# A graph network on one Trainium2 core: the adjacency products as two 64-row tiles of TensorE

## The chip, the cores and the metric

The kernel runs on one core of a Trainium2 chip. The metric is the time of the whole kernel on the device, in microseconds, median of three runs. A separate execution was recorded by the hardware profiler. Five engines work side by side: TensorE (PE in the profile, with its weight loads in a row of their own, PEld), VectorE (DVE), ScalarE (ACT), GpSimd (POOL) and SyncE (SP), which issues most of the transfers.

## The reference

The input x holds 128 graphs of 64 nodes with 256 features in 32-bit floats. One 64 x 64 adjacency matrix is shared by all graphs. Four layers follow one another, each adding to x what it makes of relu(layernorm(x)):

```python
# layer 0
h = relu(einsum('ts,bsh->bth', adj, x @ Wg0 + bg0))
h = relu(einsum('ts,bsh->bth', adj, h @ Wg1 + bg1))
for p in 1..4: an LSTM over windows of p nodes replaces the last node of each window
# layer 1
agg = einsum('nm,bmd->bnd', A_hat, features)
h = relu(batchnorm(agg @ W1.T + b1)); out = batchnorm(h @ W2.T + b2)
# layer 2
h = einsum('bjf,kfo->kbjo', x, W)
out = diag(adj) h[0] + triu(adj, 1) h[1] + tril(adj, -1) h[2] + bias
# layer 3: causal attention within a graph, with adj added to the scores
```

A_hat is the adjacency matrix with the identity added and rows and columns scaled by their degrees. The change concerns the products with adj in layer 0 (two of them) and with A_hat in layer 1.

## The kernel before

The 8192 rows (128 graphs x 64 nodes) are cut into 16 blocks of 512 rows. A block lies in on-chip memory as four groups q of 128 rows, which are two graphs each, with 256 features; features are handled as two chunks c of 128. All products are in 32-bit floats.

`aggregate` (line 180) multiplies a block by a node matrix. The matrix is held block-diagonally, 128 x 128 with the 64 x 64 matrix twice on the diagonal and zeros elsewhere (`block_diag`, line 90: `adjT_bd` for layer 0; `ahT`, line 126, for layer 1), so that one product serves two graphs. For each chunk c and each group q, line 186 takes the 128 rows of the input as the stationary operand (128 rows x 128 features) and the matrix as the moving one (128 columns). The four products of one c fill one PSUM bank, and one VectorE copy (line 187) brings the bank to `g`. The result is transposed, features on the partitions, as the next product with a weight matrix needs it. Every write starts and ends its own accumulation.

Who calls it: `graph_part` (line 229) works through layer 0's graph network for one block in five steps. The first loads x and normalises it (`layernorm_relu`, line 162: statistics on VectorE in lines 169 to 173, a power on GpSimd in line 172, four activations on ScalarE in line 176). The second makes `g0` with `aggregate`. The third multiplies by Wg0 (line 241), with an addition on VectorE (243) and a relu on ScalarE (245). The fourth makes `g1` with `aggregate`. The fifth multiplies by Wg1 (line 252), with line 255 on VectorE and 258 on ScalarE. `first_product` (line 390) does the first half of layer 1 in four steps: a load and a GpSimd copy (395); a transposition with identity (`to_token_major`, 196, with an addition on VectorE in 197), a store of the sum and the normalisation; `ag` with `aggregate`; the product with W1 (407), a ScalarE activation out of PSUM (410) and statistics on VectorE (411).

The order is written out by hand: `pipelined` (line 214) keeps one generator for each block, starts a new one in each round, and lets every live one take one step per round, the newest first. So a round of layer 0 holds, on PE's queue, `g0` of one block, line 241 of the block before, `g1` of the one before that and line 252 of the fourth, and what one step makes is used in the next round. PSUM has eight banks, handed out in turn (`bank`, line 65); a round of layer 0 and a round of layer 1 take eight each.

Between the two lies the LSTM (lines 288 to 360, the product in line 329), which takes over half of the time, and after layer 1 come layers 2 and 3 (`rest`, line 447). None of these calls `aggregate`.

Of the kernel before, what the change touches and what calls it, by code (L numbers as in the profile page):

```python
# [14 lines left out]
P = 128  # L15
# [5 lines left out]
def kernel(ctx: ExitStack, tc: tile.TileContext, a: dict, out: bass.AP):  # L21
# [4 lines left out]
    nc = tc.nc  # L26

    x = a["x"]
    B, T, D = x.shape
    NT = B * T  # L30
    KC = D // P
    SUP = 512
    NS = NT // SUP
    Q = SUP // P
# [30 lines left out]
    def bank():  # L65
        return psum.tile([P, 512], F32, tag="ps", name="ps")
# [113 lines left out]
    def aggregate(pool, h, mT, tag):  # L180

        g = pool.tile([P, KC, SUP], F32, tag=tag, name=tag)
        for c in range(KC):
            p_ = bank()
            for q in range(Q):
                nc.tensor.matmul(p_[:, ts(q, P)], h[:, q, ts(c, P)], mT, start=True, stop=True)
            nc.vector.tensor_copy(g[:, c, :], p_)
        return g

    def to_token_major(src, add, dst):  # L190
# [36 lines left out]
    with tc.tile_pool(name="pa", bufs=2) as pa, tc.tile_pool(name="pax", bufs=3) as pax:  # L227

        def graph_part(s):
            xt = pax.tile([P, Q, D], F32, tag="xt", name="xt")  # L230
            nc.sync.dma_start(xt, x_r[s])
            h = layernorm_relu(pa, xt)
            yield
            g0 = aggregate(pa, h, adjT_bd, "g0")
            yield
            h1 = pa.tile([P, Q, D], F32, tag="h1", name="h1")
# [8 lines left out]
            nc.scalar.activation(h1, h1, AF.Relu)  # L245
            yield
            g1 = aggregate(pa, h1, adjT_bd, "g1")
            yield
            for o in range(KC):
# [17 lines left out]
    with tc.tile_pool(name="wt", bufs=1) as wt:  # L267
# [5 lines left out]
        for k in range(3):  # L273
            p_ = bank().rearrange("p (d c) -> p d c", d=KC)
# [4 lines left out]
        for left, right, to in ((0, wT[:, KC : 2 * KC, :], wqk), (2, wo, wvo)):  # L279
            p_ = bank().rearrange("p (c m) -> p c m", c=KC)  # L280
            for c in range(KC):
                for d in range(KC):
                    nc.tensor.matmul(p_[:, c, :], wT[:, left * KC + d, ts(c, P)], right[:, d, :],
                                     start=(d == 0), stop=(d == KC - 1))
# [95 lines left out]
    with tc.tile_pool(name="pz", bufs=1) as pz:  # L380
# [9 lines left out]
        def first_product(s, pb, pbx):  # L390
            xt = pbx.tile([P, Q, D], F32, tag="xt", name="xt")
            nc.sync.dma_start(xt, x_r[s])
            hs = pb.tile([P, KC, SUP], F32, tag="hs", name="hs")
            for c in range(KC):
                nc.gpsimd.tensor_copy(hs[:, c, :].rearrange("p (b t) -> p b t", t=T), graphs(s, c))  # L395
            x1 = pbx.tile([P, Q, D], F32, tag="x1", name="x1")
            yield
            to_token_major(lambda c, q: hs[:, c, ts(q, P)], xt, x1)
            nc.sync.dma_start(x1d[s], x1)
            h = layernorm_relu(pb, x1)  # L400
            yield
            ag = aggregate(pb, h, ahT, "ag")
            yield
            for o in range(HC):
                p_ = bank()
                for c in range(KC):
                    nc.tensor.matmul(p_, w1[:, c, ts(o, P)], ag[:, c, :],  # L407
                                     start=(c == 0), stop=(c == KC - 1))
                z = zslot(s, o)
                nc.scalar.activation(z, p_, AF.Identity, bias=bn1[:, 0, o : o + 1])  # L410
                nc.vector.bn_stats(st1[:, o, s, :], z)
            yield
# [169 lines left out]
```

## Time and profile before

| | |
|---|---|
| median of three runs | 2158.73 us (2157.87 to 2158.78) |
| the profiled execution's own time | 2156.58 us |
| its span in the trace | 2154.9 us |
| TensorE clock granted, mean | 0.991 of full speed |
| PE busy | 2098.7 us, 97% of the span |
| VectorE busy | 791.4 us, 37% |
| ScalarE busy | 739.0 us, 34% |
| line 186, layer 0, busy on PE | 33.8 us (first product) and 31.2 us (second), 256 records each |
| line 186, layer 1, busy on PE | 43.4 us, 256 records |
| line 187, the copies, busy on VectorE | 41.4 us in layer 0, 20.4 us in layer 1 |

How to read it: the profile counts a matmul as busy from its start to its modelled end, so records of a row overlap, and the distance from start to start tells the pace. A row of groups shows line, engine, operation, what is written from what, sizes, count, busy time, mean duration, and the idle time of the engine before them with what ended it. A row of the timeline shows start, length and count of neighbouring records merged, and idle time before them in brackets. Layer 0's graph network runs from about 17 to 188 us, the first half of layer 1 from about 1385 to 1560 us.

### The profile page before, as it was taken

The page shows a single profiled execution, that of the slowest core. Times are in us where ns is not written, and L with a number is a line of the kernel's source. Part 1 is how long each engine was busy: PE and PEld are TensorE (multiplying, and loading weights), DVE is VectorE, ACT ScalarE, POOL GpSimd, SP SyncE. Part 2 cuts the span into 40 slices and gives each one's busy share as a digit, 9 for nine tenths or more (in the row PEclk, how much of TensorE's full clock was granted, in tenths as well). Part 3 has the DMA queues.
Part 4 walks back from the last instruction along what each step waited for, and adds up shares of the span by engine and source line. Part 5 has one row for each costly group of instructions (what it writes and reads, how often), then busy time and mean ns, then how long its engine had stood idle before and what let it go on. Part 6 is the DMA issues. An engine that isn't in the chain of part 4 may idle for free. (4 is left out here: it accounts for less than half of the span.)

```text
span 2154.9 us, 18142 instructions
## 1 busy us (share of the span) xinstructions
PE 2098.7 (97%) x7232; PEld 1247.9 (58%) x7232; DVE 791.4 (37%) x1569; ACT 739.0 (34%) x1267; POOL 139.2 (6%) x126
## 2 busy tenths in 40 slices
PE   6998999999999999999999999899999799999998
PEld 6775444444445666666444444455534577777777
DVE  6773222122112121122111111377634555555553
ACT  3553445233233233233222322244480133333332
POOL 1000000000000000000000000122100121111110
PEclk9999999999999999999999999999999899999999
DMA  5100000000001000000000000133200101111101
GB/s 192 58 20 20 0 0 20 0 0 0 0 0 40 0 1 0 1 0 1 0 0 0 0 0 0 59 98 98 76 0 0 41 9 40 40 40 40 40 30 40
DMA packets 35973, 54.23 MB, mean 25 GB/s; under 512 B 2608, under 2 KB 29488, under 8 KB 35888
## 3 DMA queue, kind: packets, MB, share of 16 engines
q1 hardware_dynamic: 31856, 49.29, 7.0%
q10 hardware_dynamic: 4032, 3.78, 0.6%
q8 instruction: 57, 0.93, 0.2%
q14 instruction: 28, 0.23, 0.0%
HBM read 36.28 MB, written 16.78 MB: 25 GB/s over the span
## 5 line engine op out<-in xcount | busy, mean ns | idle before, releaser
L329 PE MATMUL ps<-hT,wih 128*128 128x512 f32 (+2 forms) x2016 | 808.9, 541 | 0.0
L329 PEld LDWEIGHTS ps<-hT,wih 128*128 128x128 f32 x2016 | 383.0, 190 | 378.5 <-issue 313.3
L329 PE MATMUL ps<-hn,whh 128*128 128x512 f32 (+2 forms) x1152 | 466.3, 527 | 0.0
L329 PEld LDWEIGHTS ps<-hn,whh 128*128 128x128 f32 x1152 | 218.9, 190 | 200.4 <-issue 153.1
L176 ACT ACTIVATE ln_h<-x,ln_rn 128x256 f32<-128x256 f32 x192 | 99.7, 590 | 367.3 <-DVE ln_rn L173 362.3
L341 DVE TENSOR_TENSOR gi<-gi,gg 128x1024 f32<-128x1024 f32 (+2 forms) x36 | 38.2, 1062 | 385.6 <-ACT gg L331 385.6
L331 ACT ACTIVATE gi<-ps,lbias 128x512 f32<-128x512 f32 (+2 forms) x144 | 91.9, 638 | 234.4 <-PE ps L329 234.4
L331 ACT ACTIVATE gg<-ps,lbias 128x512 f32<-128x512 f32 (+2 forms) x144 | 91.9, 638 | 232.0 <-PE ps L329 232.0
L478 PE MATMUL ps<-wl,ag 128*128 128x256 f32 x768 | 168.4, 379 | 0.0
L478 PEld LDWEIGHTS ps<-wl,ag 128*128 128x128 f32 x768 | 144.7, 190 | 19.0
L331 ACT ACTIVATE go<-ps,lbias 128x512 f32<-128x512 f32 (+2 forms) x144 | 91.2, 634 | 89.3 <-PE ps L329 86.9
L338 DVE TENSOR_TENSOR cell<-gi,gg 128x1024 f32<-128x1024 f32 (+2 forms) x36 | 41.1, 1143 | 201.2 <-ACT gg L331 201.2
L395 POOL COPY hs<-hT 128x512 f32<-128x512 f32 x32 | 33.7, 1083 | 1228.0 <-PE ps L329 1228.0
L407 PE MATMUL ps<-ag,w 128*128 128x512 f32 x256 | 112.3, 592 | 0.0
L331 ACT ACTIVATE gf<-ps,lbias 128x512 f32<-128x512 f32 (+2 forms) x72 | 44.8, 622 | 164.9 <-PE ps L329 164.9
L342 DVE TENSOR_TENSOR cell<-gf,cell 128x1024 f32<-128x1024 f32 (+2 forms) x36 | 38.2, 1062 | 171.4 <-ACT gf L331 171.4
L172 POOL TENSOR_TENSOR ln_rn<-ln_rn,mhalf 128x4 f32<-128x4 f32 x64 | 64.6, 1009 | 565.3 <-DVE ln_rn L171 565.3
L344 ACT ACTIVATE gg<-cell 128x1024 f32<-128x1024 f32 (+1 forms) x72 | 68.7, 954 | 82.2 <-DVE cell L343 82.2
L467 PE MATMUL ps<-adj,ln_h 128*128 128x384 f32 x256 | 88.2, 499 | 6.1 <-ACT ln_h L176 6.1
L351 DVE TENSOR_TENSOR hT<-go,gg 128x512 f32<-128x512 f32 (+2 forms) x72 | 47.1, 654 | 86.7 <-ACT go L331 62.4
L407 PEld LDWEIGHTS ps<-ag,w 128*128 128x128 f32 x256 | 47.5, 190 | 54.0 <-issue 50.7
L169 DVE BATCH_NORM_STATS2 ln_st<-x 128x6 f32<-128x256 f32 x192 | 76.9, 401 | 0.0
(127 smaller groups left out, 1965.4 us busy)
## 6 DMA issues: line engine op xcount, KB each, us to landing
xt<-in_x_dram SPq DMA_DIRECT2D x32, 512.0 KB, 4.5
x1d<-x SPq DMA_DIRECT2D x16, 512.0 KB, 3.0
x<-x1d SPq DMA_DIRECT2D x16, 512.0 KB, 4.5
out_dram<-x SPq DMA_DIRECT2D x16, 512.0 KB, 3.2
wih<-in_WihT_dram SPq DMA_DIRECT2D x4, 1024.0 KB, 6.3
whh<-in_WhhT_dram SPq DMA_DIRECT2D x3, 1024.0 KB, 7.5
wqkv<-in_Wqkv_dram ACTq DMA_DIRECT2D x1, 768.0 KB, 4.2
wl<-in_W_dram ACTq DMA_DIRECT2D x3, 256.0 KB, 3.2
```

The source lines that it names most:

```text
L169: nc.vector.bn_stats(st[:, q, :], src[:, q, :])
L172: nc.gpsimd.tensor_tensor(rn[:, 0, :], rn[:, 0, :], mhalf[:, :Q], ALU.pow)
L176: nc.scalar.activation(h[:, q, :], src[:, q, :], AF.Relu, bias=rn[:, 1, q : q + 1], scale=rn[:, 0, q : q + 1])
L329: nc.tensor.matmul(o_, w[:, c, ts(m, P)], r, start=(n == 0), stop=(n == len(ops) - 1))
L331: nc.scalar.activation(gt[:, hc, :N], p_[:, :N], fn, bias=lbias[:, l, m : m + 1])
L338: nc.vector.tensor_mul(c_, i_, g_)
L341: nc.vector.tensor_mul(i_, i_, g_)
L344: nc.scalar.activation(g_, c_, AF.Tanh)
L351: nc.vector.tensor_mul(cols(blk, c, j), gate["o"][:, c, :N].rearrange("p (w b) -> p w b", b=GB), gate["g"][:, c, :N].rearrange("p (w b) -> ...
L407: nc.tensor.matmul(p_, w1[:, c, ts(o, P)], ag[:, c, :], start=(c == 0), stop=(c == KC - 1))
L467: nc.tensor.matmul(p_, h[:, q, ts(c, P)], adj3.rearrange("p k n -> p (k n)"), start=True, stop=True)
L478: nc.tensor.matmul(p_[:, q, :], ag[:, c, k, ts(q2 + q, P)], wl2[k][:, c, :], start=(n == 0), stop=(n == 3 * KC - 1))
```

## The change

The two graphs of a group are multiplied apart. The stationary operand is the 64 rows of one graph (64 rows x 128 features), the moving one the 64 x 64 block of the matrix on the same rows (64 columns). Rows 0 to 63 and 64 to 127 of the array are two tiles, and each tile writes a bank of its own[...]. A bank now holds all chunks and groups of one graph of each pair, so the two copies come after all products and write runs of 64 elements. An aggregate has 16 products in the code where it had 8, and two copies as before. In the built program 384 products stand on rows 0 to 63 and 384 on rows 64 to 127, where 384 on 128 rows stood; the order of the other instructions on each engine is the same.

```diff
@@ -180,11 +180,17 @@
     def aggregate(pool, h, mT, tag):
 
         g = pool.tile([P, KC, SUP], F32, tag=tag, name=tag)
+        half = [bank().rearrange("p (c q n) -> p c q n", c=KC, q=Q) for _ in range(2)]
+
         for c in range(KC):
-            p_ = bank()
             for q in range(Q):
-                nc.tensor.matmul(p_[:, ts(q, P)], h[:, q, ts(c, P)], mT, start=True, stop=True)
-            nc.vector.tensor_copy(g[:, c, :], p_)
+                for b in range(2):
+                    r = slice(b * T, (b + 1) * T)
+                    nc.tensor.matmul(half[b][:, c, q], h[r, q, ts(c, P)], mT[r, r],
+                                     start=True, stop=True)
+        for b in range(2):
+            to = g.rearrange("p c (q n) -> p c q n", q=Q)[:, :, :, b * T : (b + 1) * T]
+            nc.vector.tensor_copy(to, half[b])
         return g
```

## The prediction

> **What bounds the kernel now.** I read the page first (shares and slices), then the groups kept apart by shape for the lines the change touches, then one round of each stage in the timeline.
>
> ```profile
> span 2154.9 us, 18142 instructions
> PE 2098.7 (97%) x7232; PEld 1247.9 (58%) x7232; DVE 791.4 (37%) x1569; ACT 739.0 (34%) x1267; POOL 139.2 (6%) x126
> ```
>
> TensorE (PE) is busy 97% of the span, so what PE gains or loses tends to reach the end. The change touches lines 183 to 187 only, called three times for each of 16 blocks: for g0 and g1 in layer 0, for ag in layer 1.
>
> ```profile
> L186 PE MATMUL ps<-ahT,ln_h 128*128 128x128 f32 x256 | 43.4, 304 | 8.3 <-ACT ln_h L176 8.2
> L187 DVE COPY g<-ps 128x512 f32<-128x512 f32 x64 | 41.4, 682 | 1.7 <-PE ps L186 1.6
> L186 PE MATMUL ps<-adjT_bd,ln_h 128*128 128x128 f32 x256 | 33.8, 290 | 0.0
> L186 PE MATMUL ps<-adjT_bd,h 128*128 128x128 f32 x256 | 31.2, 275 | 0.0
> ```
>
> A product in the code is two MATMUL records here (256 records for 16 x 8 products), each with its own weight load. Layer 0's products never wait (0.0 idle before them), layer 1's do. One round of layer 0:
>
> ```profile
> 60.71 1.95 PE L186 MATMUL ps<-adjT_bd,h 128*128 128x128 f32 x16
> 62.49 3.60 PE L252 MATMUL ps<-g,wg 128*128 128x512 f32 x8
> 65.93 1.95 PE L186 MATMUL ps<-adjT_bd,ln_h 128*128 128x128 f32 x16
> 67.71 3.62 PE L241 MATMUL ps<-wg,g 128*128 128x256 f32 x16
> 71.17 1.95 PE L186 MATMUL ps<-adjT_bd,h 128*128 128x128 f32 x16
> ```
>
> The second column includes the last matmul's drain, so the pace is (1.95 - 0.275)/15 = 0.112 us at 128 columns, (3.62 - 0.379)/15 = 0.216 at 256, (3.60 - 0.592)/7 = 0.430 at 512: 0.83 ns for a column and about 0.004 us beside it. The round is 71.17 - 60.71 = 10.46 us, and the four groups start back to back: layer 0 is bound by PE. A round of layer 1:
>
> ```profile
> 1449.18 2.80 PE L186 MATMUL ps<-ahT,ln_h 128*128 128x128 f32 x16 [0.41 <-ACT ln_h L176]
> ...
> 1449.61 0.30 PEld L186 LDWEIGHTS ps<-ahT,ln_h 128*128 128x128 f32 x2 [0.17 <-ACT ln_h L176]
> ...
> 1451.82 7.03 PE L407 MATMUL ps<-ag,w 128*128 128x512 f32 x16
> ...
> 1458.68 1.04 PE L196 MATMUL ps<-ident,hs 128*128 128x128 f32 x8
> ...
> 1460.13 2.13 PE L186 MATMUL ps<-ahT,ln_h 128*128 128x128 f32 x10 [0.41 <-ACT ln_h L176]
> ```
>
> The round is 1460.13 - 1449.18 = 10.95 us, but PE's work in it is 16 x 0.430 + 8 x 0.109 + 16 x 0.112 = 9.54 (L196: (1.04 - 0.273)/7 = 0.109). The rest is waiting for the normalised input (L176), at the end of a loop of ScalarE and VectorE: L176, L410, L411, L197, the statistics, L173, L176. PE has 1.4 us of slack there. Layers 2 and 3 and the LSTM hold no changed instruction.
>
> The weight load row tells most. Two loads together take 0.30 us, each alone 0.19, with PE just woken from a wait: the second starts 0.11 us after the first though no stream of columns is ahead of it. [...]
>
> [...] The trace agrees on 0.11 for 128 rows; it has no 64-row load. [...] whether two loads overlap is the open point.
>
> **The change part by part.**
>
> *Matmuls.* An aggregate goes from 8 products to 16, so from 16 to 32 pairs of load and matmul. Each load still has 128 columns (the stationary is h, rows halved, columns not); each stream has 64. A stream takes 64 x 0.83 + 4 = 57 ns, now shorter than its load. Bounds: below, loads of the two tiles overlap[...]; above, loads go one after another, and none hides beside its own tile's stream[...]. I take single file loads with the streams hidden: 32 x 0.109 = 3.49 (0.109 as in L196, whose loads have 128 columns too), so +1.70 us for an aggregate. I choose this because each load is an instruction of one queue, and the trace shows loads spaced by their full time with the array empty.
>
> In layer 0 there are 32 aggregates; the first two (17.7 to 24 us, where the first rows take 6.49 us for 32 records) wait for their input and hide it. 30 x 1.70 = **+51 us**, all on the path.
>
> *Mode changes.* Each aggregate enters the tiled mode and leaves it. [...] I take half, 0.14: 60 x 0.14 = **+8 us** in layer 0 (0 to 16).
>
> *Layer 1.* PE's round becomes 9.54 + 1.70 + 2 x 0.14 = 11.52, over the loop's 10.95: 15 rounds x 0.57 = **+9 us** (4 without drains, 13 with full ones). The slack pays the rest.
>
> *Copies.* Still two of 512 elements, but into eight runs of 64. L470's VectorE copy into three runs of 128 takes 555 ns for 384 elements, L187's 680 for 512: the same slope, so I take 0; at most 0.1 each. VectorE's round in layer 0 holds about 7.6 us of work in 10.46, which hides it. Both copies now wait for the last matmul of the aggregate where the first began after half. Queued behind them on VectorE is L255 in layer 0, which itself waits for the later L252, and L411 in layer 1, where copies run some 7 us after their matmuls. Nothing is late next; were that cover gone, it would cost at most the aggregate's second half, 1.7 us a round. The consumers of g0, g1, ag come a round later.
>
> *Buffers and queues.* The second bank is claimed at the first matmul instead of the ninth. A round takes eight banks in turn, so it was emptied most of a round ago; the waits before L186 name only L176 and issue, never a copy: 0. No DMA moves.
>
> Sum: 51 + 8 + 9 = +68 on the profiled execution's 2156.6 us (span 2154.9): 2225 us. The median is 2158.7, 0.1% above; I keep to the profiled one.
>
> **The rivals.**
>
> *Loads of the two tiles overlap.* [...] Then the tile's own 16 loads bound it: no change in the matmuls, layer 1's slack covers the drains, and 60 x 0.14 = 8 remain: 2165 (2155 to 2173). Against: within a product the two loads go to one tile, and the trace never shows two loads at once.
>
> *Tiles overlap, but a load waits for its own tile's stream.* [...] +0.83 x 30 = 25, and 8: 2190.
>
> *No overlap of any kind.* +3.46 x 30 = 104, 8, and layer 1 (9.54 + 3.46 + 0.28 - 10.95) x 15 = 35: 2304. Against: the full array plainly loads behind a stream.
>
> *Faster.* Only if a 64-row load takes half as long and the tiles also run side by side: 16 x 0.057 = 0.91, -0.88 x 30 = -26, +8 for the drains, layer 1 unmoved because ScalarE and VectorE bound it: 2138. It decides once two tiles' pairs cost under 0.112 - 0.28/16 = 0.094 us together. [...]
>
> That the tiles aren't formed is no rival: the built program has 384 products on rows 0 to 63 and 384 on 64 to 127.
>
> **How the numbers follow.** Single file 0.50, overlap 0.20, half overlap 0.12, no overlap 0.12, faster 0.06. The likeliest one's own range is 2212 (no drains) to 2245 (full drains, loads spaced by 0.115). From 2157 to 2250 leaves out the faster case, the one without overlap, and a little of the second: under 2 in 10. Faster by over 0.2% (4.3 us, about what a measurement of this kernel can tell from none): 0.06 and a sliver, 0.07. Within 0.2%: the overlap case with cheap drains, 0.09. The rest, 0.84, is slower.
>
> **What would show it.** Right: 32 records in an aggregate, spaced by about 0.109 us on both PE and the loads; layer 0's round near 14.4 us; layer 1's near 11.5 with the wait for L176 gone; a gap of 0.1 to 0.3 us where an aggregate meets L241, L252 or L407; copies near 680 ns. Wrong: pairs of matmuls a few ns apart and an aggregate near 1.8 us (overlap) or 0.9 (faster); spacing of 0.16 or more (no overlap); VectorE waits growing before L255 or L411.

## The result and the profile after

The changed kernel takes 2172.86 us (median of 3, 2171.5 to 2173.9) where the kernel before took 2158.73: a ratio of 1.0067, with a 95% interval from 1.0047 to 1.0087. It is slower by 14 us; the prediction said 66 more. The direction was right and the size was not.

The page of the changed kernel, the first two lines:

```profile
span 2171.1 us, 19678 instructions
PE 2115.1 (97%) x8000; PEld 1253.7 (58%) x8000; DVE 792.6 (37%) x1569; ACT 739.0 (34%) x1267; POOL 139.1 (6%) x126
```

There are 768 more matmul records (a product in the code is two records), and the span is only 16.2 us longer. Next, one round of layer 0 in the timeline of the changed kernel, PE's matmuls (start, length, line, count):

```profile
60.67 2.00 PE L189 MATMUL ps<-adjT_bd,ln_h 64*128 64x64 f32 x32
62.60 3.72 PE L247 MATMUL ps<-wg,g 128*128 128x256 f32 x16
66.25 2.00 PE L189 MATMUL ps<-adjT_bd,h 64*128 64x64 f32 x32
68.18 3.70 PE L258 MATMUL ps<-g,wg 128*128 128x512 f32 x8
71.81 2.00 PE L189 MATMUL ps<-adjT_bd,ln_h 64*128 64x64 f32 x32
```

The aggregate has 32 records in 2.00 us, where 16 records took 1.95. Twice as many instructions need the same time. The round is 71.81 - 60.67 = 11.14 us, against 10.46 before: 0.68 for two aggregates, 0.34 for each. It sits at the borders. From the start of an aggregate to the next group is 1.93 (62.60 - 60.67) against 1.78 before, and L247's group, whose pace is unchanged, takes 3.65 until the next start (66.25 - 62.60) against 3.46. In the records from 40 to 180 us, the first load of L247 or L258 starts 0.256 us after the aggregate's last load and within 2 ns of its own matmul; in the kernel before, the first load of L241 or L252 starts 0.112 us after the last one and 0.109 ahead of its own matmul.

The weight loads of the same round:

```profile
60.67 1.86 PEld L189 LDWEIGHTS ps<-adjT_bd,ln_h 64*128 64x128 f32 x32 [0.76 <-issue]
62.60 3.32 PEld L247 LDWEIGHTS ps<-wg,g 128*128 128x128 f32 x16
```

32 loads of 0.19 us fit into 1.86. In the records one by one, loads come in twos: the load for the other tile starts 7 ns after the first, and the next two start 0.112 us later. Two loads do run at once, one in each tile. A load of 64 rows takes about as long as one of 128 (188 ns in the record against 192, and 0.112 us from one to the next of the same tile in both), so a tile does 16 loads in 16 x 0.112 us: exactly the time of the 16 full loads before. The halved streams (57 ns each by the prediction's estimate) are hidden behind them and gain nothing.

The last view is the groups of the changed kernel:

```profile
L193 DVE COPY g<-ps 128x512 f32<-128x512 f32 x64 | 41.1, 684 | 12.9 <-PE ps L189 12.9
L189 PEld LDWEIGHTS ps<-ahT,ln_h 64*128 64x128 f32 x512 | 36.2, 203 | 12.8 <-ACT ln_h L176 10.3 <-DVE ag L193 1.4 <-issue 0.5
```

A copy takes 684 ns as before (682). VectorE now waits 12.9 us in all for the products, where it waited 1.6, but VectorE isn't what bounds layer 0. In layer 1 loads wait for a copy for 1.4 us in all, which is new.

### The profile page after: what moved, and what is told of

It is laid out like the page before. It is cut to its first block, busy times and chain, and to the rows that moved or that the text cites. A ratio compares the mean times of both kernels' runs of the same rounds, so it can differ in the third digit from the quotient of the medians.

```text
span 2171.1 us, 19678 instructions
## 1 busy us (share of the span) xinstructions
PE 2115.1 (97%) x8000; PEld 1253.7 (58%) x8000; DVE 792.6 (37%) x1569; ACT 739.0 (34%) x1267; POOL 139.1 (6%) x126
## 5 line engine op out<-in xcount | busy, mean ns | idle before, releaser
L176 ACT ACTIVATE ln_h<-x,ln_rn 128x256 f32<-128x256 f32 x192 | 99.7, 589 | 365.6 <-DVE ln_rn L173 365.6
L413 PE MATMUL ps<-ag,w 128*128 128x512 f32 x256 | 118.0, 616 | 0.0
L413 PEld LDWEIGHTS ps<-ag,w 128*128 128x128 f32 x256 | 48.9, 196 | 57.7 <-issue 56.7
```

Of the source, the lines that this page charges most:

```text
L176: nc.scalar.activation(h[:, q, :], src[:, q, :], AF.Relu, bias=rn[:, 1, q : q + 1], scale=rn[:, 0, q : q + 1])
L413: nc.tensor.matmul(p_, w1[:, c, ts(o, P)], ag[:, c, :], start=(c == 0), stop=(c == KC - 1))
```

## The experiments

The theory after the result, the "drain theory": tiles load and stream side by side; the load of 128 columns sets the pace, so nothing is gained (the "load theory"); the array changes its mode (whole, or split into tiles) twice per aggregate, which costs 0.34 us, and this is the loss. A mode change is here the step from a group on all rows to a tiled one, or back; what the array does in it, and whether it drains, is not shown. The rivals: pace set by issue of instructions and not by loads; late or broken-up copies as the cost; a cost of each aggregate whatever stands beside it. Each ratio is to runs of the kernel before taken with the experiment, whose medians are 2157.6 to 2158.5 us.

**64 columns on all rows.** The same number of products and the same copies, without tiles.

```diff
-                    nc.tensor.matmul(half[b][:, c, q], h[r, q, ts(c, P)], mT[r, r],
+                    nc.tensor.matmul(half[b][:, c, q], h[:, q, ts(c, P)], mT[:, r],
```

> The 16 products of 64 columns and the late copies of the changed kernel, but each product on all 128 rows of the array (the zero block is multiplied too), so no tiles and no mode changes. Load theory [...]: an aggregate takes 32 x 0.11 = 3.5 us, +1.7 on 30 aggregates of layer 0 and about +4 us in layer 1: near 2214 us. Issue theory (a pair of load and matmul costs about 0.056 us of issue, which is what two tiles at 0.112 would also show): 32 x 0.056 = 1.8 us, no change: near 2159 us. No gap at the aggregate's borders in either.

Measured: 2238.4 us, ratio 1.0370 (1.0352 to 1.0387). A round of layer 0:

```profile
62.49 3.68 PE L189 MATMUL ps<-adjT_bd,ln_h 128*128 128x64 f32 x32
66.01 3.67 PE L247 MATMUL ps<-wg,g 128*128 128x256 f32 x16
69.52 3.68 PE L189 MATMUL ps<-adjT_bd,h 128*128 128x64 f32 x32
73.04 3.65 PE L258 MATMUL ps<-g,wg 128*128 128x512 f32 x8
76.53 3.68 PE L189 MATMUL ps<-adjT_bd,ln_h 128*128 128x64 f32 x32
```

The pace is 3.52/32 = 0.110 us for a stream of 64 columns (66.01 - 62.49 = 3.52 from start to start), nearly the same as for 128. A pair in the changed kernel took 0.056, so issue isn't the floor here, and the load of 128 columns is: the issue theory falls. This is the single file that the prediction priced, +1.74 for an aggregate (3.52 against 1.78). The total is 24 us above the expectation. Layer 0 from the first L247 to the last L258 grew by 55 us, about as expected, but what comes before it grew by 9 (the first two aggregates don't hide all of theirs), and layer 1, from its first aggregate to its last L413, by 18 in place of 4. There the granted clock was 0.50 from 1458 to 1476 us, which the expectation did not have.

**Copies alone.**

```diff
+        full = [bank() for _ in range(KC)]
         for c in range(KC):
-            p_ = bank()
...
-            nc.vector.tensor_copy(g[:, c, :], p_)
+        for c in range(KC):
+            to = g[:, c, :].rearrange("p (q b n) -> p b q n", q=Q, b=2)
+            nc.vector.tensor_copy(to, full[c].rearrange("p (q b n) -> p b q n", q=Q, b=2))
```

> Products as in the kernel before; only the copies are changed: both after all eight products, and in runs of 64 elements. Drain theory (the changed kernel's 14 us are mode changes): no change, 2159 us within 4. Copy theory (the 14 us come from late or broken-up copies): 2173 us, with waits for the copies on PE or on line 255.

Measured: 2158.3 us, ratio 1.0002 (0.9993 to 1.0010). The copies cost nothing; the copy theory falls.

**Adjacent aggregates.** The changed kernel, with the order of steps in a round of layer 0 rewritten so that both aggregates stand together on PE.

```diff
-        pipelined(map(graph_part, range(NS)), 1)
+        pipelined(map(graph_part, range(NS)), 1, [0, 1, 3, 2, 4, 5])
```

The third argument is the order in which the steps take their turn; `pipelined` sorts the live generators by it.

> The changed kernel with the two aggregates of a round of layer 0 next to each other on PE, so two mode changes in a round instead of four. Drain theory: 0.345 us less in each of 16 rounds, the round at 10.8 us, the time 5.5 us below the changed kernel's 2172.9: 2167 us. If the cost belongs to each aggregate (copies, waits, its own start), the round stays at 11.14 and the time at 2173.

Measured: 2169.2 us, ratio to the kernel before 1.0052 (1.0038 to 1.0067).

```profile
60.73 2.00 PE L189 MATMUL ps<-adjT_bd,ln_h 64*128 64x64 f32 x32
62.57 1.95 PE L189 MATMUL ps<-adjT_bd,h 64*128 64x64 f32 x32
64.45 3.72 PE L251 MATMUL ps<-wg,g 128*128 128x256 f32 x16
68.01 3.60 PE L262 MATMUL ps<-g,wg 128*128 128x512 f32 x8
71.53 2.00 PE L189 MATMUL ps<-adjT_bd,ln_h 64*128 64x64 f32 x32
```

The round is 71.53 - 60.73 = 10.80 us, as the drain theory said to the hundredth. With the same two aggregates, four mode changes gave a round of 11.14 us and two gave 10.80: the cost follows the mode changes, not the aggregates. In all, 3.7 us of the expected 5.5 were saved. By the total time alone the step from 2172.9 to 2169.2 would not be clear, since the intervals overlap; the round decides.

**The same order without tiles**, the control:

> The kernel before with the round's order of the experiment on adjacent aggregates, without tiles: a control. Drain theory: there is no mode change to save, the round stays at 10.46 us and the time at 2158 within 4. If the order itself saved time: 5 us less here too.

Measured: 2159.1 us, ratio 1.0003 (0.9995 to 1.0012): the order alone does nothing.

**Tile by tile.** All pairs of one tile, then all of the other.

```diff
-        for c in range(KC):
-            for q in range(Q):
-                for b in range(2):
+        for b in range(2):
+            for c in range(KC):
+                for q in range(Q):
```

> The changed kernel with all 16 pairs of one tile ahead of all 16 of the other on the queue. If loads of the two tiles overlap only where they stand near each other on the queue: single file, 32 x 0.112 = 3.58 us for an aggregate and 0.345 for the mode changes, about 11 us above the 2238 of the 64-column products on all rows: near 2249 us. If PE reaches past 16 pairs for the other tile: 2173 us, as the changed kernel. If it reaches some way: between.

Measured: 2251.4 us, ratio 1.0435 (1.0419 to 1.0451), near the first expectation, though not by its sum.

```profile
63.17 3.39 PE L189 MATMUL ps<-adjT_bd,ln_h 64*128 64x64 f32 x32
66.49 3.72 PE L247 MATMUL ps<-wg,g 128*128 128x256 f32 x16
```

An aggregate takes 3.39 us, not the 3.6 of pure single file. In the records one by one 12 loads are 0.112 us apart, the next seven 0.056, and the rest 0.112: near the seam, loads of the second tile go between those of the first. An estimate from the seven short spacings is that about four pairs (of a load and its matmul) of the second tile were brought forward. The overlap in the changed kernel exists because its code alternates the tiles: with that order alone changed, an aggregate takes 3.32 us to the next group's start (66.49 - 63.17) in place of 1.93. Most of what it lost beyond the products on all rows is in layer 1, where this kernel ran part of the time at half the clock, though PE was never idle; the stretches of the tile-by-tile kernel, PE's busy time first after the length, then the granted clock after POOL:

```profile
1480.00:1520.00 40.00, 40.00 (x188) 24.75 (x186) 26.33 (x57) 14.41 (x26) 9.12 (x9) 0.91 0.23 79
1520.00:1560.00 40.00, 40.00 (x195) 25.25 (x195) 27.32 (x64) 13.68 (x24) 9.08 (x9) 0.91 0.27 91
```

The products on all rows, in the same part of layer 1, kept the full clock:

```profile
1500.00:1540.00 40.00, 40.00 (x195) 25.87 (x194) 28.64 (x62) 17.92 (x32) 10.52 (x11) 1.00 0.25 82
```

From the first to the last start of L413 layer 1 took 185.1 us tile by tile and 172.3 with all rows. A round with the full clock took 11.3 us in both (1522.32 to 1533.61 tile by tile); one with a half-clock window in it took 12.95 (1509.37 to 1522.32).

**Layer 0 alone and layer 1 alone.** The changed aggregate is called in one layer and the old one in the other.

> Tiles in layer 0 alone, the aggregate of layer 1 as before. Layer 0 is bound by PE, so its 32 x 0.345 us of mode changes show in full: +11, near 2169.5 us. If the changed kernel's cost was mostly layer 1's: near 2161.

> Tiles in layer 1 alone. PE's slack of 1.4 us a round covers 0.345 in most rounds; the few early rounds of 9.53 us, which PE bounds, pay it: +1 to +3, near 2160 us. If mode changes showed in full: +5.5, 2164.

Measured: 2169.9 us, ratio 1.0057 (1.0045 to 1.0070), and 2159.7 us, ratio 1.0010 (1.0002 to 1.0018): +12.1 and +2.0, which add to the 14 of the change. Layer 1 first, two rounds of the kernel before and two of the changed kernel: an early one (from L413 to L413) and a late one.

```profile
1410.58 7.03 PE L407 MATMUL ps<-ag,w 128*128 128x512 f32 x16
...
1420.11 7.03 PE L407 MATMUL ps<-ag,w 128*128 128x512 f32 x16
```

```profile
1428.73 7.13 PE L413 MATMUL ps<-ag,w 128*128 128x512 f32 x16
...
1438.60 7.13 PE L413 MATMUL ps<-ag,w 128*128 128x512 f32 x16
...
1466.71 2.75 PE L189 MATMUL ps<-ahT,ln_h 64*128 64x64 f32 x32 [0.24 <-ACT ln_h L176]
...
1477.64 2.63 PE L189 MATMUL ps<-ahT,ln_h 64*128 64x64 f32 x29 [0.25 <-ACT ln_h L176]
```

The early round is 9.87 us against 9.53 before: PE bounds it, and it pays 0.34. The late one is 10.93 against 10.95: the wait for L176 shrank by what the mode changes took.

The first round is another matter, and by the sum of the rounds the larger part of what layer 1 pays. From the first L413 to the second it takes 12.31 us (1416.42 to 1428.73), where it took 9.53. In the changed kernel part of it runs at half the clock (0.80 is the mean over the round), in the kernel before none of it (1.00). The changed kernel first, then the kernel before; the second line of each is the round as a stretch, with the granted clock after POOL:

```profile
1416.42 9.57 PE L413 MATMUL ps<-ag,w 128*128 128x512 f32 x16
1416.40:1428.70 12.30, 12.30 (x58) 6.70 (x56) 6.43 (x12) 4.71 (x8) 3.00 (x3) 0.80 0.14 46
```

```profile
1401.05 7.03 PE L407 MATMUL ps<-ag,w 128*128 128x512 f32 x16
1401.05:1410.60 9.55, 9.55 (x43) 5.68 (x42) 6.66 (x15) 4.37 (x8) 3.04 (x3) 1.00 0.34 105
```

With tiles in layer 1 alone this round is 11.95 us; with tiles in layer 0 alone it is 9.53. The next two rounds add 0.34 and 0.06, and the fourth gives 0.9 back (10.00 against 10.94), since its waits shrink. Why the full clock comes later here is not shown.

**Four tiles of 64 x 64.** If loads set the pace, loads of 64 columns should halve it. The features are split too; the results land on the partitions where they belonged anyway.

```diff
-                    nc.tensor.matmul(half[b][:, c, q], h[r, q, ts(c, P)], mT[r, r],
-                                     start=True, stop=True)
+                    for j in range(0, P, T):
+                        nc.tensor.matmul(half[b][j : j + T, c, q],
+                                         h[r, q, c * P + j : c * P + j + T], mT[r, r],
+                                         start=True, stop=True)
```

> The changed kernel with each product split once more by feature halves: four 64 x 64 tiles, loads of 64 columns, streams of 64 columns. Load theory (a tile's own loads set the pace): a load takes 0.054 and a stream 0.056 us, 16 pairs in each tile side by side, 0.9 us for an aggregate in place of 1.79, the mode changes as they are (0.345): 32 x (-0.89 + 0.345) = -17 us against the kernel before, near 2142; layer 1 unmoved. Issue theory (0.056 us for each pair on the queue): 64 x 0.056 = 3.6 us, +2.1 an aggregate, near 2225 us.

Measured: 2145.5 us, ratio 0.9944 (0.9929 to 0.9959).

```profile
60.89 1.16 PE L190 MATMUL ps<-adjT_bd,h 64*64 64x64 f32 x64
61.98 3.70 PE L260 MATMUL ps<-g,wg 128*128 128x512 f32 x8
65.61 1.16 PE L190 MATMUL ps<-adjT_bd,ln_h 64*64 64x64 f32 x64
66.70 3.72 PE L249 MATMUL ps<-wg,g 128*128 128x256 f32 x16
70.35 1.16 PE L190 MATMUL ps<-adjT_bd,h 64*64 64x64 f32 x64
```

64 records in 1.16 us, four of them every 0.056: the load was the bound, and halving it gives the gain that the two tiles didn't. The round is 9.46 us. The total gained 12, not 17: the first blocks wait for their input (1.28 us before the second aggregate), and layer 1, from its first aggregate to its last product with W1, took 171.5 us against 169.8, where the expectation had no change.

**Tiles where the stream is longer than the load.** Layer 2's product has 384 columns, of which each graph needs 192. The kernel before, with that product alone in two row tiles:

```diff
-            for q in range(Q):
+            for q2 in range(0, Q, 2):
                 for c in range(KC):
-                    p_ = bank()[:, : 3 * P]
-                    nc.tensor.matmul(p_, h[:, q, ts(c, P)], adj3.rearrange("p k n -> p (k n)"),
-                                     start=True, stop=True)
...
+                    for q in range(2):
+                        for b in range(2):
+                            r = slice(b * T, (b + 1) * T)
+                            nc.tensor.matmul(half[b][:, q], h[r, q2 + q, ts(c, P)], adj3[r, :, r],
+                                             start=True, stop=True)
...
```

The lines left out bring the result to `ag` in eight copies of 384 elements, as many as before.

> The kernel before, with only layer 2's product (line 467, 128 rows by 384 columns, 8 a block) in two 64-row tiles with 192 columns each; eight copies of 384 elements as before. Load theory: the stream of a tile (192 x 0.83 + 4 = 0.163 us) is now longer than a load (0.112), two tiles stream side by side, so 16 x 0.163 = 2.6 us replace 16 x 0.3225 = 5.16 in each block; the two mode changes cost 0.345: 16 x (-2.55 + 0.345) = -35 us, near 2122 us. If streams of two tiles didn't overlap (the changed kernel's pace came from something else): 32 x 0.163 = 5.2 us, only the mode changes show: +5.5, near 2163 us.

Measured: 2132.4 us, ratio 0.9878 (0.9863 to 0.9893). The groups in a late round, first of the kernel before, then with the tiles:

```profile
1954.80 5.32 PE L467 MATMUL ps<-adj,ln_h 128*128 128x384 f32 x16
```

```profile
1918.99 2.87 PE L471 MATMUL ps<-adj,ln_h 64*128 64x192 f32 x32
1921.79 1.09 PE L495 MATMUL ps<-ident,ln_h 128*128 128x128 f32 x8
```

2.87 us stand where 5.32 stood, and a full round fell from 28.17 to 25.96 us: -2.21, as worked out. Here streams of two tiles do run side by side. It came to -26 and not -35 because only 12 of the 15 rounds gained; the first three went from 65.9 to 69.7 us together. In the first two of these the granted clock was 0.89 and 0.88 here and 1.00 in the kernel before.

**All of it together**, with the four tiles, adjacent aggregates and layer 2's row tiles, and then with line 526 in four tiles as well:

> Four 64 x 64 tiles in the aggregates, the two aggregates of a round adjacent, and layer 2 in two row tiles. If the parts add: 2145.5 - 5.5 - 35 = 2105 us. If they collide (waits of VectorE or ScalarE in layer 0 or 2 come forward), less is gained.

> As the kernel with three parts together, and layer 3's product of the weights with the values (line 526, the same shape as an aggregate) in four 64 x 64 tiles too; the off-diagonal weights that it leaves out are zeros. Load theory: 1.79 us become 0.9 + 0.345 in each of 16 blocks, -9 us: near 2096. If layer 3 is held by the copies out of PSUM there, which now come after all products: no gain, 2105.

Measured: 2116.9 us, ratio 0.9807 (0.9791 to 0.9824), and 2111.1 us, ratio 0.9782 (0.9767 to 0.9796). The parts add as they were measured: -12, -26 and the saved mode changes make about 2116; the expectations, with -35 for layer 2, were 2105 and 2096. The last step gave 6 of 9, its full rounds falling by 0.55 (25.96 to 25.41) as worked out. The last one is the fastest version here, 2.2% below the kernel before.

## Why the prediction was wrong, point by point

*What bounds the kernel*: right. Layer 0 pays everything that PE loses (+12.1 with tiles there alone), layer 1 little (+2.0).

*Matmuls*: this step failed. It reads "I take single file loads with the streams hidden: 32 x 0.109 = 3.49, so +1.70 us for an aggregate", on the ground that "each load is an instruction of one queue, and the trace shows loads spaced by their full time with the array empty". The spacing was read rightly, but it was the spacing of loads into the same 128 rows. It says nothing of two loads into different rows, and these start 7 ns apart in the changed kernel. The lower bound of that step, loads of the two tiles overlapping, was the truth: 16 x 0.108 to 0.112, by the spacings of loads in the kernel before, and so +0 in place of +51. The single file does exist: the tile-by-tile order has it, and the products on all rows, which came to +1.74.

*That a load sets the pace, by its columns and not its rows*: right, and the reason why the change could not gain. The runs show 0.112 us for 128 columns with 64 rows as with 128, and 0.056 for 64 columns.

*Mode changes*: 0.14 each was taken, the author's estimate, which no row of the kernel before could show; 0.17 is what the rounds show (0.34 for two). In layer 0 that is 32 x 0.34 = 11 where the prediction had 8, inside its range of 0 to 16.

*Layer 1*: +9 was predicted on a round of 11.52 us. With the loads overlapped, PE's round is 9.54 + 0.34 = 9.88, below the loop's 10.95, so the late rounds pay nothing. Of the 2.0 that came, the sum of the rounds puts most on the first one (12.31 us against 9.53), part of which ran at half the clock; the prediction has no term for the clock.

*Copies*: right; *buffers*: nearly, 1.4 us of waiting for a copy in layer 1, under its slack.

With the measured terms the sum is 0 + 11 + 2 = +13 for a measured +14. The rival "loads of the two tiles overlap", with a chance of 0.20 and a price of 2165 (2155 to 2173), was the right mechanism; 2172.9 lies at the end of its range, since it too took 8 for the mode changes and nothing for layer 1. The price for "faster" also held in its condition: two tiles' pairs had to cost under 0.094 us together, and they cost 0.112; with four tiles they cost 0.056, and the kernel became faster.

## What to carry to other kernels

Row tiles halved the stream of the block-diagonal product here, not its weight load (0.112 us with 64 rows as with 128): compare stream and load first. At 128 columns both took about 0.11 us, and the change could only lose its two mode changes (0.34 us); at 384 columns the same change gained 2.2 us a block, and at 128 it gained only once the load was split by columns too (0.056 us a load). The spacing of loads into the same rows (0.11 us) was no bound for loads into different ones (7 ns): ask what the instructions of a spacing share. When one open point decides the size and the trace cannot settle it, give its two ends comparable chances. Alternate the tiles in program order (1.93 us for an aggregate against 3.32), and put tiled groups next to each other (a round of 10.80 us against 11.14).

## What the runs showed of the hardware

In the tile-by-tile order seven of 31 spacings between loads were 0.056 us, near the seam of the two tiles, and the others about 0.11; with the tiles alternating, a load of each tile started every 0.112. A change between the full array and tiles cost 0.17 us on average in layer 0 (0.34 for the two of an aggregate). Going from one tiled group to the next cost none: with the aggregates adjacent, the second one's first load starts 0.105 us after the first one's last, the spacing inside an aggregate.

The granted clock fell to 0.91 on average over 40 us in which PE was busy all the time, in half-clock windows of 3.4 us, in layer 1 of the tile-by-tile kernel. In the changed kernel one such window lies in the middle of layer 1 (0.91 from 1500 to 1520 us, PE busy 19.55 us of 20), where the kernel before has none in the same rounds.

Near its start layer 1 ran at half the clock for 10.2 us in all in the kernel before and for 20.5 in the changed kernel, as with tiles in layer 1 alone. With the products of 64 columns on all rows it was 23.9 us, so the longer start didn't need tiles. What makes the clock fall in these stretches is not shown.
